# Two graph layers on one Trainium2 core: the first batch's adjacency, projections and scores without turn limits, and small vectors loaded as rows

## The chip, the cores and the metric

The kernel runs on one core of one Trainium2 chip. The metric is the device time of one execution in microseconds (us). The engines are named as in the profile: PE is TensorE (PEld its weight loads), DVE is VectorE, ACT is ScalarE, POOL is GpSimd, SP is SyncE. ACT and SP also issue DMAs; where their queues issue, the profile writes ACTq and SPq.

## The reference

For each of 16 batches there are 1024 nodes with 256 features `x` and a 1024 x 1024 integer adjacency `adj`. Two layers follow each other.

```python
# layer 0: 8 heads of 32, masked attention, two layer norms
q, k, v = heads(x @ Wq), heads(x @ Wk), heads(x @ Wv)
e = einsum('whqd,whkd->whqk', q, k);  e = where(e >= 0, e, 0.2 * e)
attn = softmax(where(adj > 0, e, NEG), axis=-1)
h = layernorm(attn @ v, g1, b1)
x = layernorm(concat([h, x]) @ Wffn.T, g2, b2) + x
# layer 1: two graph attentions, then a feed-forward block
def gat(h, W, a):
    Wh = h @ W
    e = leaky_relu(Wh @ a[:256] + (Wh @ a[256:]).T, 0.2)
    return softmax(where(adj > 0, e, NEG), axis=1) @ Wh
h = layernorm(x + gat(gat(x, W1, a1), W2, a2), g_ln1, b_ln1)
out = layernorm(h + relu(h @ w_ff1 + b_ff1) @ w_ff2 + b_ff2, g_ln2, b_ln2)
```

## The kernel before, in words

All work of a batch is written as small Python generators ("threads"). A planner, the class `Order`, runs them while the kernel is built: each step names an engine and a cost, each thread has an aim (a due time), and among the steps that could begin the planner takes the one with the earliest aim. The result is one fixed list of instructions for each engine; on the chip every engine works its list off in order and waits with semaphores. `take` and `give` are turns: a thread that takes from an empty pool waits until another gives. `SLOT`, 253 us, is the planned time of a batch, and the aims in `AIM` are shares of it.

The stages of a batch are these.

- `x_pair` loads 256 rows of x on ACT's queue, PE transposes them (L351), and ACT or DVE copies them into `xT`.
- `mask_part` loads adjacency pieces (L394, ACT's queue, 256 KB each), DVE converts them to fp8 (L400, `adj_b`), PE transposes them (L409) and ACT copies them into `mask` (L413). For batch 0 a part covers half of the keys, so there are 16 parts; for other batches a part has both halves.
- `qk_part` projects queries or keys of four heads (L460). ACT writes the rounded upper half (`high`, L463), DVE the remainder (`low`, L465), and SP writes both to a scratch tensor in DRAM (L469). `load_stacks` reads them back for each head as `qs` and `ks` (L543), 1 MB a head.
- `v_part` projects the values (L488).
- `all_scores` computes the scores of a head by key tile: a tile is 128 keys by 1024 queries, a head has 8 tiles, and PSUM has two tiles' room (L576, `ps_s`). `weights` turns a tile into weights `p`: 0.2 times the score (L594 on ACT, or, in batch 0 only, L592 on DVE), the maximum with the score (L596, DVE), the exponential (L599, ACT), and the product with the mask (L603, POOL).
- `all_values` multiplies pairs of `p` tiles by v (L625), and `after_head` transposes the result (L651) and divides.
- `rest` takes batch b through the remaining work while batch b + 1 has its scores: rows (L727, L730, L759), the two graph attentions (DVE writes attention rows in L812 and L815; PE multiplies in L849 and L874) and the feed-forward block (L914, L942), which reaches into a further batch.

`prepare` runs once, beside batch 0: it loads the column vectors (L288) and weights, transposes weights (L1046), multiplies the graph weights (L1052) and folds `b_ff2` into other biases (L1084).

Batch 0 has nothing before it to overlap with. Its scores are paced by `pace(0)`, which is `AIM["fast0"]` of the usual time of a pair of score tiles, and three turn pools act on it: `adj` (two mask parts at a time), `stage` (two `qk_part` at a time) and `scores` (taken twice for a pair of tiles, with one PE step for both).

Of the kernel before, what the change touches and what calls it, by code (L numbers as in the profile page):

```python
# [20 lines left out]
P = 128  # L21
# [203 lines left out]
def unshifted_path(  # L225
# [28 lines left out]
    AIM = dict(x=0.818, x_step=0, mask=0.747, mask_step=0.0264, qk0=0.614, qk1=0.898, qk_step=0.0231, v0=0.832,  # L254
# [3 lines left out]
               fast0=0.521, fast1=0.85, fast15=0.832, lead=3.15)  # L258
# [27 lines left out]
    def load_cols(v, name):  # L286
        t = const.tile([P, v.shape[0] // P], FT, name=name)
        nc.sync.dma_start(t, v.rearrange("(c p) -> p c", p=P), allow_slow_non_contiguous=True)  # L288
        return t

# [10 lines left out]
    right = const.tile([P, B, 4], FT, name="right")  # L301
    k = {}
# [80 lines left out]
    def mask_part(b, t, halves):  # L383
# [3 lines left out]
        yield take("adj")  # L387
# [15 lines left out]
        yield give("adj")  # L403
# [15 lines left out]
    def make_mask(b, t0):  # L419
        yield take("mask")  # L420
        masks[b] = buf([P, NT * N], "mask", "mask", F8)
        parts = [(t, (kh,)) for kh in range(NH) for t in range(NT)] if b == 0 else [(t, (0, 1)) for t in range(NT)]
        for n, (t, halves) in enumerate(parts):
            yield start(mask_part(b, t, halves), t0 + (AIM["mask"] + AIM["mask_step"] * n) * SLOT)
# [21 lines left out]
    def qk_part(b, g, o, nh):  # L446
# [5 lines left out]
        yield take("stage")  # L452
# [19 lines left out]
        yield give("stage")  # L472
# [38 lines left out]
    def project(b, t0):  # L511
        yield take("xT")
        xTs[b] = buf([P, DC, N], "xT", "xT")
        for u in range(NP):
            yield start(x_pair(b, u), t0 + (AIM["x"] + AIM["x_step"] * u) * SLOT)
        yield start(make_mask(b, t0), t0 + 0.5 * SLOT)
        for g in range(H // G):
            yield start(project_qk(b, g, t0 + AIM[("qk0", "qk1")[g]] * SLOT), t0)
            yield start(project_v(b, g, t0 + AIM[("v0", "v1")[g]] * SLOT), t0 + (0.8, 1.0)[g] * SLOT)
# [36 lines left out]
    def all_scores():  # L556
        for b in range(B):
# [4 lines left out]
            for h in range(H):  # L562
                yield wait(("stack", b, h))
                q, kk = stacks[b, h]
                for d in range(NT // 2):
                    due = t0 + (h * NT // 2 + d) * pace(b)
                    yield aim(due, AIM["lead"] * PACE)
                    yield take("scores")
                    yield take("scores")
                    ps = [psum.tile([P, N], FT, tag="scores", name="ps_s") for _ in range(2)]  # L570
                    yield on(PE=900)
                    for i in range(2):
                        t = 2 * d + i
                        for nh in range(NH):
                            cols = slice(nh * HALF, (nh + 1) * HALF)
                            nc.tensor.matmul(ps[i][:, cols], kk[:, t * P:(t + 1) * P], q[:, cols],  # L576
                                             start=True, stop=True)
                    if d == NT // 2 - 1:
                        yield give("stacks")
                    for i in range(2):  # L580
                        yield start(weights(b, h, 2 * d + i, ps[i]), due + i * PACE / 2)
# [428 lines left out]
    def prepare():  # L1010
# [7 lines left out]
        for name, v in (("g1c", g1), ("b1c", b1), ("g2c", g2), ("b2c", b2), ("gl1c", g_ln1), ("bl1c", b_ln1),  # L1018
                        ("bf1", b_ff1), ("bf2c", b_ff2)):
            yield load(1, 6000)  # L1020
            k[name] = load_cols(v, name)
# [33 lines left out]

        for ic in range(2 * DC):
            yield from piece(300, D, wffnT[:, ic, :], flips(wf, ic))
# [350 lines left out]
```

## Time and profile before

| what | value |
|---|---|
| median of 3 runs | 4527.06 us (4525.93 to 4528.45) |
| the profiled execution, its own time | 4521.66 us |
| its span in the profile | 4519.9 us |
| mean PE clock granted | 0.989 |
| first score matmul (L576) of batch 0 / 1 / 2 / 3 / 4 | 45.10 / 253.80 / 510.29 / 790.84 / 1061.44 us |
| a batch after that | 270.6 us |
| POOL's product with the mask (L603) | 1024 instructions, 2176 ns on average |
| DVE's maximum (L596) | 1024 instructions, 1214 ns |

The times of the first score matmul are those of every 128th matmul of L576 in the timeline; they cut the span into stages. The profile's page gives for each engine the busy time and its share of the span, then the span in 40 slices of 113 us with the busy share of each in tenths, then the chain of waits that ended last and the costliest groups of instructions. A busy engine isn't by itself the limit: what counts is which engine the others wait for in the stage concerned.

### The profile page before, as it was taken

The page shows a single profiled execution, that of the slowest core. Times are in us where ns is not written, and L with a number is a line of the kernel's source. Part 1 is how long each engine was busy: PE and PEld are TensorE (multiplying, and loading weights), DVE is VectorE, ACT ScalarE, POOL GpSimd, SP SyncE. Part 2 cuts the span into 40 slices and gives each one's busy share as a digit, 9 for nine tenths or more (in the row PEclk, how much of TensorE's full clock was granted, in tenths as well). Part 3 has the DMA queues.
Part 4 walks back from the last instruction along what each step waited for, and adds up shares of the span by engine and source line. Part 5 has one row for each costly group of instructions (what it writes and reads, how often), then busy time and mean ns, then how long its engine had stood idle before and what let it go on. Part 6 is the DMA issues. An engine that isn't in the chain of part 4 may idle for free.

```text
span 4519.9 us, 57125 instructions
## 1 busy us (share of the span) xinstructions
PE 4333.5 (96%) x20298; PEld 2875.2 (64%) x20298; DVE 3305.8 (73%) x5246; ACT 2893.4 (64%) x4030; POOL 2454.4 (54%) x1544
## 2 busy tenths in 40 slices
PE   6778999999999999999999999999999999999999
PEld 3345656667666676666667666676666767666587
DVE  4776778777787777768777787777768777776854
ACT  4556666676666666666666666666676676666631
POOL 3655665565565545655565565545655565565710
PEclk8899999999999999999999999999999999999999
DMA  6312323132232322323232232322323232231100
GB/s 177 103 49 73 89 61 109 55 88 76 59 98 64 105 60 74 91 59 110 59 86 73 59 101 68 103 64 70 90 64 102 63 88 67 62 99 49 33 22 20
DMA packets 159109, 343.57 MB, mean 76 GB/s; under 512 B 24673, under 2 KB 27233, under 8 KB 158817
## 3 DMA queue, kind: packets, MB, share of 16 engines
q1 hardware_dynamic: 112736, 255.93, 20.2%
q10 hardware_dynamic: 46080, 83.91, 6.3%
q8 instruction: 164, 2.69, 0.3%
q14 instruction: 129, 1.05, 0.1%
HBM read 239.09 MB, written 100.66 MB: 75 GB/s over the span
## 4 chain that ended last, share of the span: by engine, by line
PE 69%; DVE 17%; POOL 5%; issue 5%; ACT 3%; DMA 0%; ACTq 0%; POOLq 0%; DVEq 0%
PE ps_a L625 15%; PE ps_s L576 9%; PE ps_m L874 7%; PE ps_m L849 7%; PE ps_m L914 7%; PE ps_m L942 6%; POOL p L603 5%; DVE att L812 5%; DVE att L815 5%; DVE p L596 3%; PE ps_m L759 3%; PE ps_m L460 2%; PE ps_m L727 2%; PE ps_m L730 2%; PE ps_m L351 2%
## 5 line engine op out<-in xcount | busy, mean ns | idle before, releaser
L603 POOL TENSOR_TENSOR p<-p,mask 128x1024 f32<-128x1024 f32 x1024 | 2211.6, 2176 | 1645.2 <-ACT p L599 1521.5
L596 DVE TENSOR_TENSOR p<-p,ps_s 128x1024 f32<-128x1024 f32 x1024 | 1210.6, 1214 | 398.1 <-ACT p L594 397.3
L599 ACT ACTIVATE p<-p 128x1024 f32<-128x1024 f32 x1024 | 1081.0, 1058 | 411.6 <-DVE p L596 384.5
L594 ACT ACTIVATE p<-ps_s 128x1024 f32<-128x1024 f32 x993 | 973.6, 1025 | 183.0 <-PE ps_s L576 165.8
L625 PE MATMUL ps_a<-p,v 128*33 128x512 f32 (+1 forms) x4096 | 1005.4, 608 | 49.0 <-POOL p L603 47.6
L576 PE MATMUL ps_s<-qs,ks 128*128 128x512 f32 x2048 | 631.2, 428 | 37.1 <-DVE p L596 35.3
L576 PEld LDWEIGHTS ps_s<-qs,ks 128*128 128x128 f32 x2048 | 352.3, 191 | 338.4 <-DVE p L596 100.0
L625 PEld LDWEIGHTS ps_a<-p,v 128*33 128x33 f32 (+1 forms) x4096 | 198.1, 114 | 560.6 <-issue 398.1
L874 PE MATMUL ps_m<-y,att 128*128 128x256 f32 x2048 | 481.8, 381 | 16.3 <-ACT v L497 13.6
L942 PE MATMUL ps_m<-wf,hid 128*128 128x256 f32 x2048 | 474.0, 381 | 9.4 <-ACT xT L309 8.7
L914 PE MATMUL ps_m<-rT,wf 128*128 128x256 f32 x2048 | 474.7, 381 | 4.0 <-ACT z L309 4.0
L849 PE MATMUL ps_m<-y,att 128*128 128x258 f32 x2048 | 473.3, 381 | 2.8 <-DVE hn L658 2.8
L942 PEld LDWEIGHTS ps_m<-wf,hid 128*128 128x128 f32 x2048 | 379.3, 190 | 78.7 <-issue 15.7
L849 PEld LDWEIGHTS ps_m<-y,att 128*128 128x128 f32 x2048 | 386.4, 190 | 66.8 <-issue 6.0
L874 PEld LDWEIGHTS ps_m<-y,att 128*128 128x128 f32 x2048 | 376.3, 190 | 81.5 <-ACT v L497 16.3
L812 DVE SCALAR_TENSOR_TENSOR att<-first,second 128x1024 f32<-128x1024 f32 x256 | 352.8, 1378 | 81.9 <-ACT first L799 81.9
L914 PEld LDWEIGHTS ps_m<-rT,wf 128*128 128x128 f32 x2048 | 378.4, 190 | 52.9 <-ACT z L309 4.3
L815 DVE SCALAR_TENSOR_TENSOR att<-mask,att 128x1024 f32<-128x1024 fp8e4 x256 | 329.9, 1289 | 8.7
L820 ACT ACTIVATE y<-y,check 128x258 f32<-128x258 f32 x256 | 130.8, 511 | 303.4 <-DVE check L818 283.6
L334 POOL TENSOR_SCALAR rs<-mv 128x2 f32<-128x2 f32 (+1 forms) x224 | 58.8, 262 | 392.5 <-DVE mv L331 392.4
L400 DVE TENSOR_SCALAR adj_b<-adj_i 128x512 fp8e4<-128x512 int32 x256 | 249.4, 1019 | 15.5 <-DMA adj_i<-in_adj_dram 15.5
L923 ACT ACTIVATE hid<-ps_m,bf 128x256 f32<-128x256 f32 x383 | 163.5, 471 | 128.6 <-PE ps_m L914 101.0
(100 smaller groups left out, 4254.7 us busy)
## 6 DMA issues: line engine op xcount, KB each, us to landing
adj_i<-in_adj_dram ACTq DMA_DIRECT2D x256, 256.0 KB, 3.4
qs<-qk_halves SPq DMA_DIRECT2D x256, 256.0 KB, 4.1
ks<-qk_halves SPq DMA_DIRECT2D x256, 256.0 KB, 5.1
qk_halves<-high SPq DMA_DIRECT2D x128, 256.0 KB, 3.2
qk_halves<-low SPq DMA_DIRECT2D x128, 256.0 KB, 3.6
xr<-in_x_dram ACTq DMA_DIRECT2D x64, 256.0 KB, 2.8
x_kept<-x SPq DMA_DIRECT2D x64, 256.0 KB, 2.0
x<-x_kept SPq DMA_DIRECT2D x64, 256.0 KB, 5.4
```

The lines of the kernel that those rows point to most:

```text
L576: nc.tensor.matmul(ps[i][:, cols], kk[:, t * P:(t + 1) * P], q[:, cols], start=True, stop=True)
L594: nc.scalar.activation(p, ps, AF.Copy, scale=ALPHA)
L596: nc.vector.tensor_tensor(p, p, ps, op=OP.max)
L599: nc.scalar.activation(p, p, AF.Exp)
L603: nc.gpsimd.tensor_tensor(p, p, mask_of(b, t), op=OP.mult)
L625: nc.tensor.matmul(acc[nh * 64:nh * 64 + m, :], v[:, t, c:c + m], p[:, nh * HALF:(nh + 1) * HALF], start=(t == 0), stop=(t == NT - 1))
L812: nc.vector.scalar_tensor_tensor(e, first[:, 0, :], second[:, j:j + 1], first[:, 1, :], op0=OP.mult, op1=OP.max)
L815: nc.vector.scalar_tensor_tensor(e, mask_of(b, j), -1.0, e, op0=OP.mult, op1=OP.mult, accum_out=sums[:, j:j + 1])
L849: nc.tensor.matmul(pa[:, cols:cols + width], big[:, j, i * P:(i + 1) * P], rows[:, j, :width], start=(j == 0), stop=(j == NT - 1))
L874: nc.tensor.matmul(pa[:, i * D:(i + 1) * D], big[:, j, t * P:(t + 1) * P], y2[:, j, :D], start=(j == 0), stop=False)
L914: nc.tensor.matmul(pa[:, i * 2 * P:(i + 1) * 2 * P], wf1[:, dc, hc * P:(hc + 1) * P], rT[:, dc, :], start=(dc == 0), stop=(dc == DC - 1))
L942: nc.tensor.matmul(pa[:, i * D:(i + 1) * D], hid[hc // 2][:, hc % 2, i * P:(i + 1) * P], wf2[:, hc, :], start=(hc == 0), stop=False)
```

## The change

The diff does the following. For batch 0 it takes away the turn pools `adj` and `stage`, so that all mask parts and all projections of that batch can be under way at once, as far as buffers go. A mask part of the second key half waits for the same tile's first half instead. The aims of batch 0's own x loads and of `make_mask` move to the very beginning; its mask parts get an aim of their own, `mask0` (0.6 in place of 0.747), and `fast0` falls from 0.521 to 0.4. All other aims and all costs stay. Scores of batch 0 are taken and issued by single tiles (`n = 1`), those of other batches by pairs as before. The eight small vectors no longer land as columns in eight tiles (`load_cols`): each is loaded as rows of 128 numbers into the spare end of `setup`, PE transposes the 22 rows at once, and one copy puts them into `columns`, of which the vectors are slices.

```diff
@@ -251,11 +251,11 @@
     PACE = SLOT / (H * NT // 2)
 
 
-    AIM = dict(x=0.818, x_step=0, mask=0.747, mask_step=0.0264, qk0=0.614, qk1=0.898, qk_step=0.0231, v0=0.832,
+    AIM = dict(mask0=0.6, x=0.818, x_step=0, mask=0.747, mask_step=0.0264, qk0=0.614, qk1=0.898, qk_step=0.0231, v0=0.832,
                v1=0.974, v_step=0.0591, rows=-0.244, rows_step=0.0408, first0=0.12, first1=0.252,
                graph0=-0.009, graph1=0.21, graph_step=0, second=0.355, second_step=0.0335, normed=0.78,
                normed_step=0.026, ff_wait=(None, 0, 1, 0), ff=(0.532, -0.011, 0.487, 0.497), ff_step=0.0386,
-               fast0=0.521, fast1=0.85, fast15=0.832, lead=3.15)
+               fast0=0.4, fast1=0.85, fast15=0.832, lead=3.15)
 
     const = ctx.enter_context(tc.tile_pool(name="const", bufs=1))
     sb = ctx.enter_context(tc.tile_pool(name="sb", bufs=1))
@@ -283,11 +283,6 @@
         nc.sync.dma_start(dst, w.rearrange("(c p) o -> p c o", p=P))
         return dst
 
-    def load_cols(v, name):
-        t = const.tile([P, v.shape[0] // P], FT, name=name)
-        nc.sync.dma_start(t, v.rearrange("(c p) -> p c", p=P), allow_slow_non_contiguous=True)
-        return t
-
     def load_row(v, name):
         t = const.tile([P, v.shape[0]], FT, name=name)
         nc.sync.dma_start(t, bass.AP(tensor=v.tensor, offset=v.offset, ap=[[0, P], [1, v.shape[0]]]))
@@ -299,6 +294,7 @@
     wf2 = const.tile([P, HC, D], FT, name="wf2")
     w12 = const.tile([P, DC, YW + 2], FT, name="w12")
     right = const.tile([P, B, 4], FT, name="right")
+    columns = const.tile([P, 32], FT, name="columns")
     k = {}
 
 
@@ -384,7 +380,10 @@
 
         n = len(halves)
         ints = []
-        yield take("adj")
+        if b:
+            yield take("adj")
+        elif halves[0]:
+            yield wait(("mask", b, t, 0))
         for kh in halves:
             yield take("pair")
             ai = buf([P, HALF], "pair", "adj_i", I32)
@@ -400,7 +399,8 @@
             nc.vector.tensor_scalar(ab[:, i * HALF:(i + 1) * HALF], ai, 0.0, -1.0,
                                     op0=OP.is_gt, op1=OP.mult, saturate=False)
             yield give("pair")
-        yield give("adj")
+        if b:
+            yield give("adj")
         yield take("misc")
         pt = misc(BF)
         pairs = ab.bitcast(BF)
@@ -421,7 +421,7 @@
         masks[b] = buf([P, NT * N], "mask", "mask", F8)
         parts = [(t, (kh,)) for kh in range(NH) for t in range(NT)] if b == 0 else [(t, (0, 1)) for t in range(NT)]
         for n, (t, halves) in enumerate(parts):
-            yield start(mask_part(b, t, halves), t0 + (AIM["mask"] + AIM["mask_step"] * n) * SLOT)
+            yield start(mask_part(b, t, halves), t0 + (AIM["mask" if b else "mask0"] + AIM["mask_step"] * n) * SLOT)
 
     def mask_of(b, t):
 
@@ -449,7 +449,8 @@
         cols = slice(nh * HALF, (nh + 1) * HALF)
         for u in range(nh * 2, nh * 2 + 2):
             yield wait(("xT", b, u))
-        yield take("stage")
+        if b:
+            yield take("stage")
         yield take("pair")
         yield take("pair")
         yield take("misc")
@@ -469,7 +470,8 @@
             nc.sync.dma_start(scratch[b, g][o, :, i, cols], part)
         yield give("pair")
         yield give("pair")
-        yield give("stage")
+        if b:
+            yield give("stage")
         yield fire(("qk", b, g, o, nh))
 
     def project_qk(b, g, t0):
@@ -512,8 +514,8 @@
         yield take("xT")
         xTs[b] = buf([P, DC, N], "xT", "xT")
         for u in range(NP):
-            yield start(x_pair(b, u), t0 + (AIM["x"] + AIM["x_step"] * u) * SLOT)
-        yield start(make_mask(b, t0), t0 + 0.5 * SLOT)
+            yield start(x_pair(b, u), t0 + (AIM["x"] + AIM["x_step"] * u if b else 0.0) * SLOT)
+        yield start(make_mask(b, t0), t0 + (0.5 if b else 0.0) * SLOT)
         for g in range(H // G):
             yield start(project_qk(b, g, t0 + AIM[("qk0", "qk1")[g]] * SLOT), t0)
             yield start(project_v(b, g, t0 + AIM[("v0", "v1")[g]] * SLOT), t0 + (0.8, 1.0)[g] * SLOT)
@@ -562,23 +564,23 @@
             for h in range(H):
                 yield wait(("stack", b, h))
                 q, kk = stacks[b, h]
-                for d in range(NT // 2):
-                    due = t0 + (h * NT // 2 + d) * pace(b)
+                n = 2 if b else 1
+                for t in range(0, NT, n):
+                    due = t0 + (h * NT + t) / 2 * pace(b)
                     yield aim(due, AIM["lead"] * PACE)
-                    yield take("scores")
-                    yield take("scores")
-                    ps = [psum.tile([P, N], FT, tag="scores", name="ps_s") for _ in range(2)]
-                    yield on(PE=900)
-                    for i in range(2):
-                        t = 2 * d + i
+                    for _ in range(n):
+                        yield take("scores")
+                    ps = [psum.tile([P, N], FT, tag="scores", name="ps_s") for _ in range(n)]
+                    yield on(PE=450 * n)
+                    for i in range(n):
                         for nh in range(NH):
                             cols = slice(nh * HALF, (nh + 1) * HALF)
-                            nc.tensor.matmul(ps[i][:, cols], kk[:, t * P:(t + 1) * P], q[:, cols],
+                            nc.tensor.matmul(ps[i][:, cols], kk[:, (t + i) * P:(t + i + 1) * P], q[:, cols],
                                              start=True, stop=True)
-                    if d == NT // 2 - 1:
+                    if t + n == NT:
                         yield give("stacks")
-                    for i in range(2):
-                        yield start(weights(b, h, 2 * d + i, ps[i]), due + i * PACE / 2)
+                    for i in range(n):
+                        yield start(weights(b, h, t + i, ps[i]), due + i * PACE / 2)
 
     def weights(b, h, t, ps):
         yield take("p")
@@ -1015,10 +1017,17 @@
         def part(i, n):
             return setup[:, i * 512:i * 512 + DC * n].rearrange("p (c n) -> p c n", c=DC)
 
-        for name, v in (("g1c", g1), ("b1c", b1), ("g2c", g2), ("b2c", b2), ("gl1c", g_ln1), ("bl1c", b_ln1),
-                        ("bf1", b_ff1), ("bf2c", b_ff2)):
-            yield load(1, 6000)
-            k[name] = load_cols(v, name)
+
+        vectors = (("g1c", g1), ("b1c", b1), ("g2c", g2), ("b2c", b2), ("gl1c", g_ln1), ("bl1c", b_ln1),
+                   ("bf1", b_ff1), ("bf2c", b_ff2))
+        lines = sum(v.shape[0] // P for _, v in vectors)
+        at = 0
+        for name, v in vectors:
+            n = v.shape[0] // P
+            yield load()
+            nc.sync.dma_start(setup[at:at + n, 2620:2620 + P], v.rearrange("(c p) -> c p", p=P))
+            k[name] = columns[:, at:at + n]
+            at += n
         for name, v in (("gl2", g_ln2), ("bl2", b_ln2)):
             yield load()
             k[name] = load_row(v, name)
@@ -1053,6 +1062,9 @@
                                      start=(fc == 0), stop=(fc == DC - 1))
             return emit
 
+        yield from piece(200, lines, columns[:, :lines],
+                         lambda pt: nc.tensor.transpose(pt[:, :lines], setup[:lines, 2620:2620 + P],
+                                                        ident[:lines, :lines]))
         for ic in range(2 * DC):
             yield from piece(300, D, wffnT[:, ic, :], flips(wf, ic))
         wTs = []
```

## The prediction

> **What bounds the kernel now.** I read the page's busy shares and its 40 slices first: is one engine full, and where not?
>
> ```profile
> PE 4333.5 (96%) x20298; PEld 2875.2 (64%) x20298; DVE 3305.8 (73%) x5246; ACT 2893.4 (64%) x4030; POOL 2454.4 (54%) x1544
> ...
> PE   6778999999999999999999999999999999999999
> ...
> PEclk8899999999999999999999999999999999999999
> ```
>
> PE is full except in the first three slices (340 us), so only the opening can give time cheaply. Next I cut the timeline at the first score matmul (L576) of each batch and asked for the busy times between the cuts (columns: stretch, length, then busy us of PE, PEld, DVE, ACT, POOL, then PE clock, DMA share, GB/s).
>
> ```profile
> 0.00:45.10 45.10, 27.59 (x134) 17.66 (x135) 10.80 (x23) 13.64 (x29) 1.38 (x12) 0.98 0.68 208
> 45.10:253.80 208.70, 159.40 (x598) 65.36 (x599) 146.03 (x147) 115.47 (x139) 132.67 (x64) 0.85 0.41 113
> 253.80:510.29 256.49, 216.81 (x965) 130.04 (x965) 181.66 (x277) 165.78 (x216) 146.07 (x86) 0.95 0.26 71
> 510.29:790.84 280.55, 271.07 (x1273) 178.07 (x1273) 210.27 (x324) 189.14 (x267) 160.73 (x97) 0.99 0.29 84
> 790.84:1061.44 270.60, 266.96 (x1266) 178.37 (x1264) 204.20 (x325) 182.31 (x253) 152.38 (x97) 1.00 0.28 79
> ```
>
> From the fourth stretch on each batch takes 270.6 us and PE is busy 267: a change to batch 0 can't touch that. In batch 0's scores (208.7 us) no engine is full: PE 159 at a clock of 0.85, DVE 146, POOL 133. What lies between is waiting. The timeline of that stretch shows the usual cycle and the worst hole:
>
> ```profile
> 137.32 1.20 PE L576 MATMUL ps_s<-qs,ks 128*128 128x512 f32 x4
> 138.17 1.23 DVE L592 TENSOR_SCALAR p<-ps_s 128x1024 f32<-128x1024 f32 x1 [0.43 <-PE ps_s L576]
> 139.88 2.34 DVE L596 TENSOR_TENSOR p<-p,ps_s 128x1024 f32<-128x1024 f32 x2
> 142.50 1.20 PE L576 MATMUL ps_s<-qs,ks 128*128 128x512 f32 x4
> ...
> 73.74 2.12 POOL L603 TENSOR_TENSOR p<-p,mask 128x1024 f32<-128x1024 f32 x1 [12.03 <-PE ps_m L460]
> ...
> 91.65 5.30 DVE L400 TENSOR_SCALAR adj_b<-adj_i 128x512 fp8e4<-128x512 int32 x4
> ```
>
> Two score tiles go as one pair: PE fills both, DVE works both off (1.23 + 2.34), and only then does PE fill two again. A pair comes every 5.2 us (137.32 to 142.50), 2.6 a tile, though POOL needs 2.135 (median of L603 here). At 73.74 POOL had waited 12.0 us because the second half of the mask wasn't there. The list of waits of this stretch totals it for DVE:
>
> ```profile
> DVE p L592 <- PE ps_s L576: 41.0, 24, 5.4
> ...
> DVE p L596 <- ACT p L594: 11.5, 4, 6.1
> ```
>
> **What the Trainium skill says.** "SBUF — State Buffer", section "SBUF: two separate sides": the port pair that DVE and GpSimd share is an exclusive lock held for a whole instruction. The trace agrees: a conversion L400 takes 0.42 us in the opening, where POOL is idle, and 5.30 for four (1.32 each) at 91.65, where POOL works. "TensorE: Matmul & The Clock Gate", section "What's actually happening": an idle window halves the PE clock. It agrees: the clock is 0.50 from 45 to 60 us, 1.00 in the dense stretches. "DMA: Bandwidth & Descriptors", section "Rules for kernel authors": a strided last dimension becomes one descriptor per element. It agrees with the column vectors: g1c, 1 KB, needs 7.6 us to land, more than any of the 256 KB loads' medians in the first 60 us but one.
>
> **The change part by part.** The instruction order of both kernels is fixed at build, so I compared them engine by engine. PE and POOL have the same sequence in batches 6 to 15, and at the first score of batch 4 PE has done exactly the same matmuls in both, but for one transpose more. So the difference is the time at which batch 4 begins (1061.44 us now); from there it is a shift. The tail differs only in which of ACT and DVE evacuates a few tiles: nothing, since PE covers it.
>
> *Opening, to the first score.* ACT's queue now issues the 4 x loads first and then 8 adjacency loads in a row. x lands about 3 us earlier; ACT's own work waits behind the 12 issues, which at the start go about as fast as bytes move (four x issues took 4.51 us). All 16 mask parts now stand on PE ahead of the first score (11 before), and SP has all 16 writes of high/low ahead of the first stack load (12 before). Five parts cost PE 0.28, ACT 0.38 and DVE 0.42 each; no engine is full here (PE 27.6 of 45). What counts is bytes: three more adjacency loads (13 were issued before the first score until now) and 4 more writes, 7 x 0.26 MB = 1.8 MB, at the 240 GB/s measured from 35 to 45 us: +7.7. Less the 3 us of the earlier x: **+4** (bounds -2, all hidden, to +10).
>
> *The mask hole.* With every mask part ahead of the scores the 12.0 us go: **-12** (bounds -6, if POOL then waits for late exponentials, to -12). Late next is ACT: it still issues batch 1's x and adjacency loads between its exponentials; between 46.4 and 51.6 us three x issues held it for 5.2 us. That is in both kernels.
>
> *Conversions.* Five of the 21 L400 leave batch 0's stretch for the opening, where POOL doesn't hold the port: 5 x 1.32 = **-6.5** of DVE time (bounds 0 to -6.5).
>
> *Scores by single tiles.* A tile's buffer is free after its own maximum (L596, 1.21), so PE refills it (0.6) while DVE is on the other. DVE then needs, per tile, 1.21 and for 28 of 64 tiles also 1.23: 1.75; POOL's 2.135 is the slower. 64 x 2.135 = 137 for POOL; for DVE 64 x 1.21 + 28 x 1.23 + 16 x 1.32 + 8 low x 0.69 + 12 for heads and copies = 150. One of 208.7 is left, so at most 59 can go in all. PE still has products (L625) that wait for POOL in order ahead of the next scores, but in the new order four score tiles are under way by then, over 8 us of POOL's work. I take two thirds of the 41.0 us that DVE waited for scores: **-27** (bounds 0 and -41). The third that stays is head changes, batch 1's projections ahead in PE's queue and half-clock stretches.
>
> *Aims.* fast0 falls from 0.521 to 0.40 and mask0 to 0.6. They act only through the order already compared; their cost is in the items above.
>
> *Vectors as rows.* Eight SP issues stay eight; 2816 single elements become 22 rows of 512 B. One transpose and one copy of 22 columns come in, each under 0.4 us like the pieces beside them. SP isn't late for anything but stacks, whose loads are 4 to 10 us for a head of 18: **0**; if that cover is gone, up to 2 either way.
>
> *bf2's product (L1084).* Its 16 tiny matmuls, 4.26 us on PE and 4.10 on the chain of waits, move with the two large weight loads from batch 0 into batch 1: -4 there, +2 here (PE is busy 82% where it lands): **-2** (bounds -4 to +2).
>
> *Batches 1 to 3.* They took 807.6 us with 52.8 idle on PE and have the same PE work after. The order is new: batch 0's attention now lies about one head later against batch 1's scores. In the old order PE fell to 20.9 busy of 32 (317 to 349 us) and 19.9 of 32 (413 to 445) while DVE made attention rows; the new one has as many scores or more there. I take **0** (bounds -15 to +25).
>
> Sum: 4 - 12 - 6.5 - 27 - 2 + 0 = **-43.5**. Against the profiled execution (4519.9 us span, 4521.66 with what lies around) that is 4478.2. The median of the runs, 4527.06, is 5.4 above that execution, so the forecast is **4483.5**.
>
> **The rivals.**
> (a) *DVE, not the pairing, bounds batch 0.* For it: DVE was 146 us busy of 208.7, and conversions hold it in blocks of four. Against: 41 us of waits on scores. Then only the hole and the conversions come: 4 - 12 - 6.5 - 2 = -16.5, 4510.5. Chance 0.12.
> (b) *Batches 1 to 3 give it back.* This is the slower end. The two attention stages of a batch leave PE about 11 and 12 us idle in batch 1, since no feed-forward work fills them; in batches 2 and 3 it does (idle 9.5 and 3.6). If the new order opens both holes in batches 2 and 3 too, that costs 2 x 23 = 46, and a longer one in batch 1 adds 12: -43.5 + 58 = +14.5, 4541.5. It decides from 43.5 us of idle time more than now. For it: the aims for batches 1 and on were set for the old start. Against: feed-forward pieces do stand between the attention steps in the new order of batch 2. Chance 0.10.
> (c) *Nothing to see.* Score tiles go singly but PE's order (products waiting for POOL) keeps the old cycle, and the opening takes +10: the hole's 12 us are all eaten. 4525, chance 0.05.
> The main case has 0.73; up to 60 us can go in it, so it reaches from 4460 to 4503.
>
> **How the numbers follow.** About 0.2% (9 us) is what a measurement of this kernel tells from no change. Main case and (a) are faster, 0.85; (c) is 0.05; (b) 0.10. The range takes in the main case and (a): 4458 to 4514.
>
> **What would show it.** In the changed kernel's trace: first score at 49 us (right if 43 to 55); no POOL gap near 12 us after it; L605 at steps near 2.2 to 2.5 a tile; batch 1's first score at about 210 us instead of 253.8; batches 1 to 3 together 808 us; then 270.6 each. If batch 1 begins later than 235, the pairing was not the limit. If it begins near 210 and the end doesn't move by as much, (b) is right.

## The result, and the profile after

The changed kernel takes 4530.55 us (median of 20 runs, 4526.06 to 4534.75), the kernel before, on the same chip, 4525.98 us (20 runs, 4519.42 to 4531.72). The ratio is 1.001, with a 95% interval of 1.0004 to 1.0017: no change by the prediction's bound of about 0.2%, and if anything slower. The forecast was 4483.5, with 4458 to 4514 as the range. Stages below are read from one profiled execution of each kernel.

The page of the changed kernel (engine, busy us, share; then tenths by slices of 113 us) shows nearly the same shares as that of before. Two rows tell something: PE's first slices rise from 677 to 788, and the clock's second slice is 9 where it was 8, while its third, which now lies in batch 1, is 8 where it was 9.

```profile
PE 4352.1 (96%) x20299; PEld 2889.7 (64%) x20299; DVE 3338.5 (74%) x5265; ACT 2888.7 (64%) x4012; POOL 2469.0 (54%) x1544
...
PE   7888999999999999999999999999999999999998
...
PEclk8989999999999999999999999999999999999999
```

The stretches between the first score matmuls (L578 now) of batches 0 to 4 say where the time went. This is the same division as in the prediction, for the changed kernel:

```profile
0.00:44.09 44.09, 29.74 (x145) 19.09 (x145) 13.12 (x28) 14.98 (x34) 1.38 (x12) 0.97 0.82 266
44.09:214.43 170.34, 141.94 (x557) 58.54 (x558) 144.87 (x140) 115.62 (x136) 133.04 (x65) 0.91 0.40 113
214.43:493.05 278.62, 241.00 (x1014) 142.49 (x1013) 193.07 (x275) 166.73 (x216) 163.47 (x90) 0.89 0.28 79
493.05:790.45 297.40, 274.71 (x1255) 180.64 (x1253) 223.56 (x338) 181.24 (x250) 164.33 (x94) 0.97 0.26 73
790.45:1068.30 277.85, 268.59 (x1271) 178.35 (x1269) 214.28 (x335) 180.28 (x246) 152.05 (x96) 1.00 0.27 77
```

| stretch | before | after | difference |
|---|---|---|---|
| opening | 45.10 | 44.09 | -1.0 |
| batch 0's scores | 208.70 | 170.34 | -38.4 |
| batch 1 | 256.49 | 278.62 | +22.1 |
| batch 2 | 280.55 | 297.40 | +16.9 |
| batch 3 | 270.60 | 277.85 | +7.2 |
| batches 4 to 14 | 2976.34 | 2976.87 | +0.5 |
| from batch 15's first score to the end | 482.1 | 487.0 | +4.9 |

Batch 1 begins 39.4 us earlier, close to the forecast. Batches 1 to 3 then take 46.2 us more and give it all back. (The two profiled executions differ by 12.2 us in span, the medians by 4.6: the slow end of one kernel's runs is compared with the fast end of the other's.)

**What is different inside batches 1 to 3.** While batch b has its scores, `rest` makes the two graph attentions of batch b - 1. Each has eight attention rows on DVE (L814 and L817, L812 and L815 before); one such group of eight is called a stage here. In the old order the rows stand together in five of the six stages of batches 1 to 3. DVE's timeline of the kernel before, in batch 1 (start, us, instruction):

```profile
316.05 1.23 DVE L815 SCALAR_TENSOR_TENSOR att<-mask,att 128x1024 f32<-128x1024 fp8e4 x1
...
317.40 1.26 DVE L812 SCALAR_TENSOR_TENSOR att<-first,second 128x1024 f32<-128x1024 f32 x1
318.70 1.22 DVE L815 SCALAR_TENSOR_TENSOR att<-mask,att 128x1024 f32<-128x1024 fp8e4 x1
...
320.04 1.26 DVE L812 SCALAR_TENSOR_TENSOR att<-first,second 128x1024 f32<-128x1024 f32 x1
321.34 1.22 DVE L815 SCALAR_TENSOR_TENSOR att<-mask,att 128x1024 f32<-128x1024 fp8e4 x1
```

A row every 2.65 us (316.05, 318.70, 321.34). In the new order the rows of all four stages of batches 1 and 2 stand in turn with score tiles (those of batch 3 stand together, as before). From the changed kernel's timeline of the same stage:

```profile
280.18 2.13 POOL L605 TENSOR_TENSOR p<-p,mask 128x1024 f32<-128x1024 f32 x1 [1.66 <-ACT p L601]
280.24 3.15 DVE L817 SCALAR_TENSOR_TENSOR att<-mask,att 128x1024 f32<-128x1024 fp8e4 x1
...
283.52 1.22 DVE L598 TENSOR_TENSOR p<-p,ps_s 128x1024 f32<-128x1024 f32 x1
...
284.79 1.22 PE L578 MATMUL ps_s<-qs,ks 128*128 128x512 f32 x2 [4.11 <-DVE p L598]
...
285.96 2.13 POOL L605 TENSOR_TENSOR p<-p,mask 128x1024 f32<-128x1024 f32 x1 [3.65 <-ACT p L601]
285.97 3.20 DVE L817 SCALAR_TENSOR_TENSOR att<-mask,att 128x1024 f32<-128x1024 fp8e4 x1
```

POOL's product begins at 280.18 and DVE's L817, started 0.06 us later, lasts 3.15 us instead of 1.22: it ends about 1 us after the product. Behind it on DVE stands the tile's maximum (L598, 283.52); PE waited 4.11 us for that before it could make the next score, and POOL 3.65 us for its exponential. So everything goes at one row and one tile in 5.73 us (280.24 to 285.97). "SBUF — State Buffer", section "SBUF: two separate sides", of the Trainium skill says that the port which DVE and GpSimd share is an exclusive lock; the 1.22 against 3.15 us agree with it. The groups of batch 1 (columns: count, then busy us, mean ns, idle us before) give the sum, before and after:

```profile
L815 DVE SCALAR_TENSOR_TENSOR att<-mask,att 128x1024 f32<-128x1024 fp8e4 x16 | 19.6, 1224 | 0.5
```

```profile
L817 DVE SCALAR_TENSOR_TENSOR att<-mask,att 128x1024 f32<-128x1024 fp8e4 x16 | 39.9, 2495 | 0.6
```

From first to last row a stage of batch 1 then takes 41 and 42 us instead of 19. In score tiles that loses little: seven tiles pass in the first of them, which at the 2.85 us of a tile in a head without rows (22.8 us for 8) are 20 us. But the chain behind the rows is late. Second rows, second attention, norm and feed-forward follow the rows one after the other, so the last attention row begins 225 us after batch 1's first maximum instead of 169. Its products then come when the batch's scores are used up. The changed kernel's timeline at the end of batch 1, and the busy times of this stretch (columns as above):

```profile
472.49 1.22 DVE L598 TENSOR_TENSOR p<-p,ps_s 128x1024 f32<-128x1024 f32 x1 [0.22 <-ACT p L596]
...
480.72 3.62 PE L876 MATMUL ps_m<-y,att 128*128 128x256 f32 x16
...
493.05 1.18 PE L578 MATMUL ps_s<-qs,ks 128*128 128x512 f32 x4
```

```profile
472.49:496.88 24.39, 24.33 (x135) 19.27 (x132) 11.71 (x32) 6.74 (x10) 6.14 (x9) 1.00 0.29 90
```

From 472.49 to batch 2's first maximum at 496.88 DVE has no score tile: 24.4 us, where the kernel before has 6.2 at this place. This hole is not itself the loss. PE works through all of it at full clock, on products that were left over; and the order before has longer holes in batch 1, 26.5 us in each of its two stages, where PE has less to do (16.6 us busy of the 29.8 around the first).

**What PE loses.** In batches 1 to 3 PE idles 69.6 us instead of 52.8, which is 16.8 of the 46.2. The clock is the larger part. The trace's clock record holds only full and half speed: half speed covers 61 us of batch 1 (27 before) and 20 us of batch 2 (3 before), and PE was busy for 68 us of that in all, against 19 before. The median record of a values matmul (L627, 512 columns) is 592 ns at full and 1061 ns at half speed. By these two, an estimate: 44% of the busy time at half speed is loss, 30 us against 8, or 22 us more than before. What is left of the 46.2, some 8 us, is mostly other PE work that moved in, 4.2 us of it bf2's product (L1096). In batch 1 alone PE idles no more than before (37.6 us, before 39.7): what it loses there is clock and moved work, not idle time.

### The profile page after: what moved, and what is told of

The parts are those of the page before. It is cut to its first block, busy times and chain, and to the rows that moved or that the text cites. A ratio compares the mean times of both kernels' runs of the same rounds, so it can differ in the third digit from the quotient of the medians.

```text
span 4532.1 us, 57096 instructions
## 1 busy us (share of the span) xinstructions
PE 4352.1 (96%) x20299; PEld 2889.7 (64%) x20299; DVE 3338.5 (74%) x5265; ACT 2888.7 (64%) x4012; POOL 2469.0 (54%) x1544
## 4 chain that ended last, share of the span: by engine, by line
PE 68%; DVE 19%; POOL 5%; issue 4%; ACT 3%; DMA 0%; SPq 0%; ACTq 0%; POOLq 0%; DVEq 0%
PE ps_a L627 15%; PE ps_s L578 9%; PE ps_m L876 8%; PE ps_m L851 7%; PE ps_m L916 7%; PE ps_m L944 6%; DVE att L817 5%; DVE att L814 5%; POOL p L605 4%; DVE p L598 4%; PE ps_m L461 3%; PE ps_m L761 2%; PE ps_m L729 2%; PE ps_m L732 2%; PE ps_m L347 2%
## 5 line engine op out<-in xcount | busy, mean ns | idle before, releaser
L598 DVE TENSOR_TENSOR p<-p,ps_s 128x1024 f32<-128x1024 f32 x1024 | 1210.8, 1213 | 407.9 <-ACT p L596 406.4
L596 ACT ACTIVATE p<-ps_s 128x1024 f32<-128x1024 f32 x996 | 976.6, 1024 | 202.8 <-PE ps_s L578 185.7
L627 PE MATMUL ps_a<-p,v 128*33 128x512 f32 (+1 forms) x4096 | 999.1, 605 | 28.6 <-POOL p L605 27.6
L578 PE MATMUL ps_s<-qs,ks 128*128 128x512 f32 x2048 | 640.4, 432 | 54.5 <-DVE p L598 51.3
L578 PEld LDWEIGHTS ps_s<-qs,ks 128*128 128x128 f32 x2048 | 353.7, 192 | 358.2 <-DVE p L598 118.3
L627 PEld LDWEIGHTS ps_a<-p,v 128*33 128x33 f32 (+1 forms) x4096 | 198.5, 113 | 532.5 <-issue 399.7
L814 DVE SCALAR_TENSOR_TENSOR att<-first,second 128x1024 f32<-128x1024 f32 x256 | 354.0, 1383 | 73.1 <-ACT first L801 73.1
L817 DVE SCALAR_TENSOR_TENSOR att<-mask,att 128x1024 f32<-128x1024 fp8e4 x256 | 363.3, 1419 | 8.7
L925 ACT ACTIVATE hid<-ps_m,columns 128x256 f32<-128x256 f32 x373 | 159.5, 471 | 118.5 <-PE ps_m L916 92.8
```

The costliest lines, as they stand in the source:

```text
L578: nc.tensor.matmul(ps[i][:, cols], kk[:, (t + i) * P:(t + i + 1) * P], q[:, cols], start=True, stop=True)
L596: nc.scalar.activation(p, ps, AF.Copy, scale=ALPHA)
L598: nc.vector.tensor_tensor(p, p, ps, op=OP.max)
L627: nc.tensor.matmul(acc[nh * 64:nh * 64 + m, :], v[:, t, c:c + m], p[:, nh * HALF:(nh + 1) * HALF], start=(t == 0), stop=(t == NT - 1))
L814: nc.vector.scalar_tensor_tensor(e, first[:, 0, :], second[:, j:j + 1], first[:, 1, :], op0=OP.mult, op1=OP.max)
L817: nc.vector.scalar_tensor_tensor(e, mask_of(b, j), -1.0, e, op0=OP.mult, op1=OP.mult, accum_out=sums[:, j:j + 1])
```

## The experiments

In the expectations, theory A is that the rows in turn with score tiles make batches 1 to 3 longer; B is that PE itself loses the time, because it waits for POOL's products and its clock halves; C is A's later form, that each stage in turn has a price wherever it lies. A stage is called in turn below where its rows follow at more than 3.3 us a row, together where they follow at 2.65 to 2.93. Runs without a number of executions were run once.

**Rows held together in batch 1 (dense_rows).** The changed kernel with one more turn: in batch 1 no POOL product may be placed between the rows of a stage. (The last `...` stands before the start of a row; not shown are that the other rows wait for the one that took the turn, and that the last row gives it back.)

```diff
+        if 0 < b <= 1:
+            yield take("port")
         yield on(POOL=2050, shared=True)
         nc.gpsimd.tensor_tensor(p, p, mask_of(b, t), op=OP.mult)
+        if 0 < b <= 1:
+            yield give("port")
...
+        if b < 1:
+            if j == 0:
+                yield take("port")
```

> The changed kernel, but in batch 1's stretch the planner lets no product with the mask (POOL) of batch 1 begin between the 8 attention rows of each of batch 0's two attentions, so that DVE's order has the rows together. Nothing else is edited. Theory A (batch 0's gain is eaten because DVE makes attention rows in turn with score tiles: 5.9 us a row where the old kernel has 2.66, and the chain through both attentions sets batch 1's end): rows 2.7 us apart, batch 1 about 250 us instead of 279, L817's sum in it about 21 us instead of 41, the kernel 20 to 35 us faster than the changed one (about 4500). Theory B (PE itself loses the time: its order in batch 1 makes it wait for POOL's products, and its clock halves): rows close up, but batch 1 stays above 270 us and the kernel within 10 us of the changed one.

Measured: 4536.94 us (20 runs), ratio 1.002 (1.0013 to 1.0027). The rows did come at 2.93 and 2.65 us, and L817 with its read-outs took 22.9 us in all instead of 41.2, but the batch only went from 278.6 to 273.1 us.

```profile
215.38:488.43 273.05, 233.93 (x1026) 139.04 (x1025) 185.63 (x283) 169.96 (x220) 150.90 (x90) 0.91 0.30 84
488.43:781.27 292.84, 271.41 (x1258) 178.92 (x1256) 217.44 (x327) 181.81 (x252) 159.81 (x93) 0.98 0.25 71
781.27:1073.81 292.54, 273.17 (x1256) 180.64 (x1255) 220.96 (x328) 180.50 (x249) 157.82 (x98) 0.98 0.26 72
```

Theory A's numbers were missed, and B's came true: the rows close up, batch 1 stays above 270 us, and the kernel is within 10 us of the changed one (6.4 slower). The edit re-laid the whole order: batch 2 has two stages in turn, batch 3 now one, and batch 3 takes 292.5 us instead of 277.9. Within batch 1 the rows begin later (71 us after its first maximum; 64 in the changed kernel, 59 before), and the clock stays low (0.91). Why batch 1 is not shorter, with both stages together, is not explained by theory A.

**POOL's products made short, with both orders kept (short_pool_after, short_pool_before).** In batches 1 and 2 the product with the mask covers 64 of 1024 columns; the rest of these weights stays unmasked, and the lower limit of the softmax sums is opened to fit. No planned cost is changed, so each order stays as it was.

```diff
-        nc.gpsimd.tensor_tensor(p, p, mask_of(b, t), op=OP.mult)
+        w = 64 if b in (1, 2) else N
+        nc.gpsimd.tensor_tensor(p[:, :w], p[:, :w], mask_of(b, t)[:, :w], op=OP.mult)
```

> The changed kernel, its order untouched; in batches 1 and 2 POOL multiplies only 64 of 1024 columns of each tile by the mask, so that it holds the port it shares with DVE for a short time (the other columns' weights stay unmasked in those two batches, and the lower limit of the sums that are counted at the end is opened to fit). Lock alone (part of theory A): the second step of a row, L817, falls from 41 to about 21 us in sum in batch 1 and likewise in batch 2; batch 1 loses 15 to 25 of its 279 us, batch 2 10 to 15 of 297. If the interleaving with score tiles, not the lock, is what costs: batch 1 loses under 8.

> The same edit in the kernel before (64 columns of POOL's product in batches 1 and 2, the rest unmasked, limit of the sums opened). Its rows in batch 1 already lie together: theory A expects batch 1 to lose under 8 of 256 us and batch 2 up to 8 of 281. Theory B expects as much as in the changed kernel, since PE waits for POOL's products in both.

Measured: 4475.82 and 4499.84 us. Batches 1, 2 and 3 with the new order, then with the old one:

```profile
213.66:457.81 244.15, 225.01 (x1015) 135.65 (x1013) 161.62 (x275) 165.97 (x216) 47.30 (x90) 0.96 0.33 90
457.81:729.31 271.50, 264.53 (x1256) 177.75 (x1253) 184.66 (x338) 181.50 (x250) 42.77 (x94) 0.99 0.28 80
729.31:1008.88 279.57, 270.34 (x1270) 179.50 (x1268) 214.39 (x335) 180.47 (x246) 150.32 (x96) 0.99 0.27 77
```

```profile
252.09:494.82 242.73, 213.96 (x965) 130.48 (x965) 162.20 (x278) 167.22 (x217) 33.88 (x87) 0.95 0.27 73
494.82:766.32 271.50, 268.25 (x1274) 177.56 (x1272) 178.96 (x322) 188.20 (x266) 41.77 (x98) 1.00 0.31 89
766.32:1037.25 270.93, 267.18 (x1267) 178.48 (x1265) 204.17 (x325) 182.30 (x253) 150.05 (x95) 1.00 0.28 78
```

With short products both orders need nearly the same time in batches 1 and 2 (244.2 and 242.7; 271.5 and 271.5). The new one loses 10.1 us over batches 1 to 3 instead of 46.2, and is 24.0 us faster at the end. So of the 39.0 us that it loses in batches 1 and 2 nearly all (37.6) needs POOL's full product; batch 3, whose products are full in both runs, keeps its loss (8.6 us, with full products 7.2) although its rows stand together, and that part is open.

As a test of A against B the pair is undecided. The new order gained 34.5 and 25.9 us in batches 1 and 2, the old one 13.8 and 9.1: each more than A's ranges, and not the same in both orders, as B had it.

The changed order's rows are still in turn here (4.1 to 4.8 us a row), the last one still begins late (193 us after batch 1's first maximum, 162 in the old order), and the hole at the end of batch 1 is still there:

```profile
437.27:461.63 24.36, 24.30 (x135) 19.27 (x132) 11.71 (x32) 6.74 (x10) 3.05 (x8) 1.00 0.41 105
```

So with short products neither the turn nor the late chain costs the time. The attention row's second step (L817, line 818 in this file) is back at 1.24 us on average in batch 1: its length came from POOL's products. The run does not tell this hold on DVE from POOL's own time, which fell from 163 to 47 us busy in batch 1.

**Pairs in place of single tiles (pairs_after).** The changed kernel with `n = 2` for batch 0 too.

> The changed kernel with batch 0's score tiles in pairs again (n = 2 for all batches), all else as changed. The prediction's step of -27 us for single tiles: batch 0's stretch from the first score to batch 1's first score about 195 to 200 us instead of 170. If the missing limits on mask parts did most of it: under 180. The later batches have another order, so the kernel's end says nothing here; only batch 0's stretch is read.

Measured: 4701.09 us in all, since this order does not settle (its batches come to no fixed length): batches 4 to 9 take 285 to 296 us each. For the question only batch 0 counts:

```profile
45.42:231.54 186.12, 148.07 (x590) 60.80 (x590) 143.20 (x145) 113.30 (x133) 133.42 (x65) 0.90 0.42 116
```

It is 15.8 us longer than with single tiles (170.34) and 22.6 shorter than before (208.70): between the two ranges that were expected.

**One number of the planner (fast0_55, fast0_521, fast0_35_fast1_8).** The changed kernel with other aims for the pace of the scores, which change nothing but the order. The third run also lowers `fast1`, from 0.85 to 0.8.

```diff
-               fast0=0.4, fast1=0.85, fast15=0.832, lead=3.15)
+               fast0=0.55, fast1=0.85, fast15=0.832, lead=3.15)
```

> The changed kernel with one number edited: fast0 = 0.55 instead of 0.4. Its order leaves batch 0's part much as it is and, in DVE's list, puts the 8 rows of each of batch 0's attentions together again in batch 1, as the kernel before has them. After dense_rows I hold theory C: the time is lost wherever, in batches 1 to 3, attention rows stand in turn with score tiles (before has one such stage of six, the changed kernel four, dense_rows three in other batches); each costs some 10 to 15 us beyond a stage with its rows together. C expects batch 1 to begin at 215 to 222 us, rows 2.65 us apart in both stages of batch 1, batch 1 about 250, batch 2 about 278, batch 3 271, and the kernel near 4480 (4470 to 4490), 40 us faster than before. Rival D, that a shorter batch 0 is always paid back because batches 1 to 3 have no room for it: batch 4 still begins at 1060 or later, the kernel at 4520 or more.

> The changed kernel with fast0 at its old value, 0.521. Batch 0's stretch as in the changed kernel (about 170 us), but by DVE's order the rows of both of batch 0's attentions, and of both of batch 1's, are in turn with score tiles. Theory C: four such stages as in the changed kernel, so the gain of batch 0 is lost again: 4515 to 4535. If the value of fast0 mattered by itself and not by the order of the rows, this kernel would lie near fast0_55.

> The changed kernel with fast0 = 0.35 and fast1 = 0.8. By DVE's order only one of the six attention stages of batches 1 to 3 has its rows in turn with score tiles, as in the kernel before. Theory C: batch 1 begins near 213, batches 1 to 3 take about 800 us together, the kernel 4465 to 4490. Rival D: 4520 or more. It differs from fast0_55 in the way fast0 moves (down, not up), so that agreement of the two speaks for the rows and against the aim itself.

Measured: fast0 = 0.55 gives 4490.68 us (4 runs), ratio to the kernel before 0.9919 (0.9902 to 0.9936); 0.35 with fast1 = 0.8 gives 4491.15, ratio 0.9916 (0.9899 to 0.9933); 0.521 gives 4527.05, as expected. The first two beat both kernels, by 0.8%. Batches 0 to 3 with 0.55:

```profile
45.65:216.32 170.67, 140.59 (x558) 57.34 (x558) 142.23 (x140) 115.10 (x135) 134.02 (x65) 0.92 0.46 126
216.32:473.86 257.54, 221.46 (x998) 134.00 (x996) 181.83 (x279) 164.85 (x215) 145.19 (x86) 0.95 0.25 69
473.86:753.81 279.95, 271.10 (x1273) 177.88 (x1273) 210.06 (x324) 189.22 (x267) 161.05 (x97) 0.99 0.30 84
753.81:1024.43 270.62, 266.87 (x1267) 178.39 (x1265) 203.88 (x325) 182.39 (x253) 152.52 (x97) 1.00 0.28 78
```

Batch 0 is as short as in the changed kernel, and batches 1 to 3 take 808.1 us, as before the change (807.6), with one stage in turn, as before. The lead of 37.5 us at batch 1 is 37.0 at batch 4. So a shorter batch 0 need not be paid back. With 0.35 and 0.8 it is much the same: batch 1 begins at 215.8, batches 1 to 3 take 812.0 us with one stage in turn. Both kernels lie about 1 us above the times expected (4490 at most).

**Two neighbours (fast0_56, fast0_53).** The same line with 0.56 and 0.53.

> The changed kernel with fast0 = 0.56, one hundredth above the best one so far. In its order the attention rows of batches 1 and 2 stand together, and both stages of batch 3 stand in turn with score tiles. Theory C (stages in turn cost the time, wherever they lie): batch 1 about 257 us, batch 2 about 274, batch 3 about 292; the loss moves to batch 3, and the time is 4497 to 4512. Rival E (what counts is fast0 itself, that is when batch 1 begins against its aims; the curve is smooth): like 0.55, batch 3 at 270.6 and 4485 to 4495.

> The changed kernel with fast0 = 0.53, two hundredths below the best one so far. In its order all four attention stages of batches 1 and 2 stand in turn with score tiles, and those of batch 3 stand together. Theory C: batches 1 to 3 take 840 to 855 us in all (808 with 0.55), and the time is 4518 to 4535. Rival E (smooth in fast0, between 4527 at 0.521 and 4487 at 0.55): near 4514 or less.

Measured: 4512.78 us with 0.56 (C expected 4512 at most) and 4525.56 with 0.53 (as C expected). Batches 1 to 3 with 0.56:

```profile
214.88:480.83 265.95, 229.49 (x1027) 137.25 (x1025) 185.33 (x281) 169.98 (x223) 149.86 (x90) 0.93 0.26 70
480.83:754.36 273.53, 262.98 (x1231) 172.15 (x1229) 209.75 (x328) 179.15 (x246) 147.12 (x92) 0.99 0.28 81
754.36:1045.65 291.29, 277.87 (x1300) 185.85 (x1298) 212.93 (x327) 183.60 (x256) 165.59 (x97) 0.99 0.26 74
```

Most of the loss lies in batch 3 now, where rows stand in turn (6.49 and 5.85 us a row), and batch 2, with both stages together, takes 273.5. That is where C put it and where nothing smooth in fast0 would. Batch 1, at 265.9, is 9 us over C's number although both its stages stand together. 0.53 and 0.521 give the same stages within 0.2 us (276.5, 291.6, 272.5, in all 840.6), and 0.55, two hundredths more, takes 32.5 us less for them.

**Single tiles and fast0 alone (singles_only).** The kernel before with `n = 1` for batch 0 and fast0 = 0.4.

> The kernel before with two edits alone: batch 0's score tiles one by one (n = 1) and fast0 = 0.4; the turns for mask parts and halves, the column vectors and all other aims as before. The prediction gave single tiles 27 us and the mask parts 12 + 6.5: batch 1 begins at about 227 instead of 253.8. By DVE's order batches 1 and 2 have their rows together, and both stages of batch 3 are in turn: theory C expects some 20 us to be lost there, the kernel at 4505 to 4520.

Measured: 4534.8 us; missed. Batch 0 gives 22.3 us (186.40 for 208.70), batch 1 begins 21.7 us earlier, and batch 3, with both stages in turn (6.77 and 5.85), takes 293.4 us, 22.8 more than before, as C had it. C did not have that batch 1 takes 263.8 us with its rows together (before 256.5), nor that the tail is 5.7 us longer. Batch 2, with none in turn, takes 274.0 (before 280.5).

**The vectors alone (rows_alone).** The kernel before with the part of the change that loads vectors as rows (as in the diff above).

> The kernel before with the vectors as rows alone, nothing else of the change. The prediction's step: 0, up to 2 us either way; batch 1's first score at 252 to 256 us, batch 4's at 1059 to 1064, the ratio within 0.1% of 1. Rival: the eight row loads or the transpose hold up the opening or the weights behind them on SP's queue; then the first score or batch 1's start is later by 5 us or more and the kernel slower by over 0.1%.

Measured: 4526.08 us (12 runs), ratio 0.9999 (0.999 to 1.0008); batch 1 begins at 254.62, batch 4 at 1062.53. No difference, as the step said.

**The limits put back (limits_back).** The changed kernel with the turns `adj` and `stage` for batch 0 too.

```diff
-        if b:
-            yield take("adj")
-        elif halves[0]:
-            yield wait(("mask", b, t, 0))
+        yield take("adj")
...
-        if b:
-            yield take("stage")
+        yield take("stage")
```

> The changed kernel with the turn limits adj and stage of batch 0 put back; aims, single tiles and rows as changed. The prediction's steps for the mask hole and the conversions (-12 and -6.5): batch 0's scores take 18 us longer than in the changed kernel, about 189 us, with a hole of about 12 us on POOL near the beginning. Rival: with single tiles the limits no longer matter, 170 to 175 us. For batches 1 to 3, theory C: four of six stages stand in turn in the order (the first of each batch, and both of batch 3), so they take 840 to 855 us together, though nothing of the change touches them.

Measured: 4719.44 us, from an order that does not settle. Its opening and batch 0, and then three batches with none, two and one of their stages in turn (5, 6 and 8):

```profile
0.00:35.26 35.26, 25.93 (x121) 17.13 (x121) 8.01 (x17) 12.05 (x25) 1.39 (x12) 0.98 0.69 219
35.26:228.44 193.18, 156.57 (x614) 64.44 (x614) 149.92 (x153) 117.79 (x144) 133.82 (x65) 0.89 0.48 131
1367.89:1639.98 272.09, 263.08 (x1239) 173.89 (x1237) 201.05 (x330) 179.50 (x243) 154.14 (x98) 1.00 0.27 77
1639.98:1939.86 299.88, 282.01 (x1310) 188.86 (x1309) 220.12 (x336) 181.08 (x250) 163.42 (x98) 0.98 0.25 73
2229.23:2514.12 284.89, 269.41 (x1262) 178.25 (x1261) 214.16 (x328) 182.21 (x251) 161.91 (x97) 0.99 0.26 75
```

POOL's timeline (its product is L599 in this file) has the hole of before at the same place; the changed kernel has no gap over 1 us in its first eleven products:

```profile
74.27 8.38 POOL L599 TENSOR_TENSOR p<-p,mask 128x1024 f32<-128x1024 f32 x4 [11.68 <-ACT mask L409]
```

Batch 0 is 22.8 us longer with the limits (18 expected) but the first score comes 8.8 us earlier (35.26 for 44.09); together the limits cost 14.0 us at batch 1's start. Batches 1 to 3, with four stages in turn, take 854.4 us, as C expected.

**All batches together.** Batches 2 to 14 of all kernels here that compute everything (before, after and ten others, 156 batches), sorted by how many of their two stages stand in turn:

| stages in turn | batches | mean length | from - to |
|---|---|---|---|
| 0 | 129 | 271.5 us | 270.3 - 287.4 |
| 1 | 11 | 285.9 us | 279.9 - 298.1 |
| 2 | 16 | 292.4 us | 284.3 - 299.9 |

So the first stage in turn goes with 14 us, the second with 7 more. The long ones with none (283 to 287) are all in the two orders that never settle; there even the batches with none average 279.5 us. In the ten orders that settle the means are 270.9 (119 batches), 283.0 (5) and 293.0 (6). This goes together; it doesn't show a cause, since the orders differ in more than their rows and most of the batches with none repeat one settled order. In batch 1, which the table leaves out, the tie is loose: 256 to 273 us with none in turn (7 kernels), 265 with one, 269 to 279 with two (4 kernels).

## Why the prediction was wrong

- *Opening, +4: -1.0.* (7.7 less 3 is nearer to 5.) Both terms were there, and one was small. The limits' removal costs 8.8 us (7.7 taken from the bytes). The earlier x and masks, taken as 3, are worth more: the first score is at 45.74 with the old aims and limits (singles_only) and at 35.26 with the new aims and limits (limits_back), 10.5 less.
- *Mask hole and conversions, -12 and -6.5:* right in mechanism; with limits against without, batch 0 differs by 22.8 us (18.5 forecast).
- *Single tiles, -27:* over-sized. Beside the rest of the change they are worth 15.8 us, by themselves with fast0 22.3. The step took two thirds of the waits from the kernel before, but single tiles and the lifted limits seem to take up some of the same waits: they give 22.6 and 22.3 apart and 38.4 together.
- *Vectors as rows, 0:* right. *Aims of batch 0, 0:* wrong twice over: those of x and the masks give some 10.5 us, and with fast0 alone edited batches 1 to 3 take 808 to 854 us.
- *bf2's product, -2:* not measured alone. Its 16 matmuls (32 records) lie in batch 1 now and take 4.2 us of PE there (4.3 in batch 0 before); PE is busy all the time where they land, so the +2 was too small. Batch 0 has 41 records fewer: these 32, and 10 of mask transposes that went into the opening, less one of the vectors' transpose.
- *Batches 1 to 3, "I take 0 (bounds -15 to +25)": the step that failed.* It was +46.2, outside its bounds. The step looked at whether PE would have scores to do in the attention stages, and found as many or more. They were there. It did not ask what these scores do to the rows, that DVE's rows, POOL's products and the maxima then wait for each other; and it put PE's clock at nothing, though the clock was 0.95 in batch 1 and PE idle for 39.7 us there. The first reading, that PE is full after three slices, had passed over the 8 in the fourth, which is batch 1. (The batches of 270.6 us begin with the fifth stretch, not the fourth.)
- *Batch 1's start, about 210: 214.4.* That this is right to 4 us is in part luck: the opening came out 5 us better and the limits 4 us better than forecast, and single tiles 5 to 11 us worse.
- *Tail, nothing:* +4.9 us in the profiled execution; it takes 482 to 494 us in the orders here, and no run tells why.

Rival (b) had the outcome: batch 1 near 210 (214.4) and an end that does not move. That its 46 us for two holes equals the 46.2 measured is chance. It wanted idle PE time, 23 us more in each of batches 2 and 3 and 12 in batch 1; idle time grew by 13.2 and 5.6 us in batches 2 and 3 and fell by 2.1 in batch 1. The rest is PE work at a lower clock (0.89 for 0.95 in batch 1, 0.97 for 0.99 in batch 2) and the work that was moved. Its point for it, that the aims of batches 1 and on were set for the old start, weighed more than the feed-forward pieces counted against it.

What is shown: the loss lies in batches 1 to 3; it comes from their new order and not from the shorter batch 0, since fast0 = 0.55 keeps batch 0's gain without it; and in batches 1 and 2 nearly all of it needs POOL's full product. What is argued: that the rows in turn are what costs in that order. The lengths of batches 2 to 14 go with it, but the one run that closed the rows up in batch 1 gained 5.5 of its 22 us. The late chain is not enough by itself, as the short products show. Open: how the loss divides between the hold on DVE's rows, POOL's own time and PE's clock; why batch 1 of dense_rows is long; batch 3 of the changed kernel; and the tail.

## What to carry to other kernels

Where one fixed order comes out of a planner, a gain at the start is not a shift of the rest: compare the new order in the first stages after it, and for each group of instructions on the longest chain ask what now stands between them and at what clock PE will run, not only whether PE has work there. Rows of a serial chain that share a port with another engine's long instructions are worth a look: here the second step of a row went from 1.22 to 2.50 us on average in batch 1. Closing them up by force in one batch was no cure, since the later order moved too. And when an aim or a pace is re-tuned, read the order before the time: 0.53, 0.55 and 0.56 gave 4526, 4491 and 4513 us.

## What was not expected of the hardware

Two DVE instructions of the same shape are held by POOL quite differently. L817, with both inputs in SBUF, goes from 1.22 us alone to 3.0 to 3.2 where a POOL product has just begun; the maximum L598, whose second input is the score tile in PSUM, averages 1.21 us in batch 1 of either kernel (1214 and 1213 ns), though POOL is busy for more than half of that time. It works the other way too: in the changed kernel a POOL product that begins while DVE has a row (291.72) takes 3.08 us instead of 2.13.
